# A two-stage graph network on one core: layer 0 taken over its edge blocks as a pipeline, its loads two blocks early, its stores on GpSimd's queue, the first norm ahead of the branch

## The chip, the cores and the metric

The kernel runs on one core of a Trainium2 chip. A core has a matrix engine (TensorE, PE in the profile), a vector engine (VectorE, DVE), a scalar engine (ScalarE, ACT), a general engine (GpSimd, POOL) and a queue engine (SyncE, SP). They work through their own instruction streams in order and wait for each other by semaphores. SBUF is the on-chip memory with 128 partitions, PSUM holds the results of matmuls, and transfers run on 16 shared DMA engines, issued from SP, ACT or POOL. The metric is the device time of one execution in microseconds (us); lower is better.

## The reference

There are 6250 nodes with 64 features and 206250 directed edges, sorted by target node. First a simple graph layer (layer 0) is applied to the normalised nodes, then three attention layers (the transformer convolution) to the normalised result, each with a residual:

```python
h = jnp.maximum(_layernorm(x, axis=-1), 0.0)
# layer 0: a message per edge from the target's own row, mean by target
x_i = x[dst]
msg = jax.nn.relu(jnp.concatenate([x_i, edge_attr], axis=-1) @ W1 + b1)
summed = jax.ops.segment_sum(msg, dst, num_segments=N)
count = jax.ops.segment_sum(jnp.ones(...), dst, num_segments=N)
aggr = summed / jnp.maximum(count, 1.0)[:, None]
out = jax.nn.relu(aggr + (x @ Wres + bres))
# attention, three times (2, 2 and 1 heads)
q = x @ Wq + bq;  k = x @ Wk + bk;  v = x @ Wv + bv
e = eattr @ We
alpha = jnp.sum(q[dst] * (k[src] + e), axis=-1) / jnp.sqrt(C)
m = jax.ops.segment_max(alpha, dst, num_segments=n)
a = jnp.exp(alpha - m[dst])
a = a / (jax.ops.segment_sum(a, dst, num_segments=n)[dst] + 1e-16)
out = jax.ops.segment_sum(a * (v[src] + e), dst, num_segments=n) + x @ Ws + bs
```

Between the attention layers stands a PReLU. All data is float32.

## The kernel before

The edges are padded to 206848 and cut into 101 windows (`NW`) of 2048 edges (`WE`), each of 4 chunks of 512 edges. As edges are sorted by target, the targets of a window lie within 128 consecutive nodes, those of a chunk within 32. `gnn_kernel` checks this on the chip (L94 to L126: `cur` and `prev` hold the target of each edge and of the edge before it, one window per partition, so 101 partitions), writes two tables (`lrow`, an edge's node within its chunk, and `starts`, where a new node begins) to DRAM, and branches: `windows` when the edges fit, which is what runs here, `general` otherwise.

`windows` first makes constants: index rows, `dl` (target within the chunk), block-diagonal weights `w0blk` and `wblk`, the tables of padding rows. Then the norm of x and its projection run over all 49 node blocks of 128 (L311 to L349); the results go to DRAM as `qt[0]` (the projected row, split into three bf16 parts) and `st[0]` (residual and x).

The loop of layer 0 (L357 to L426) goes over the 101 windows. In each: `ea`, the edge features for four windows, is loaded every fourth window (L361); the copy `ead` rearranges the attention's edge features from DRAM to DRAM (L365); `lb` brings `lrow` on 96 partitions (L369), `load_q` the rows of the window's chunks from `qt[0]` (L296), `rx` residual and x (L372). A one-hot matrix `ohT` is made of `lb` (L374) and stored as `ohd` for the attention layers (L375). For two halves of the window, PE forms the messages in `pm` (edge part L380, node part L383), ACT takes the Relu (L387), and PE sums them by node in `acc` with the one-hot `oh` (L389, L400). `nodes` orders the sums by node (L302 to L308), the last node of a window is carried to the next by a matmul with `last` (L393). Then come mean, residual and second norm on DVE and ACT (L405 to L424), and `project` (L275 to L289) makes k, v, q and the skip row and stores them on SP as `kvt`, `qt` and `st`, next to x1 as `x1t` (L411). After the loop `masks` (L235 to L256) makes scans from `starts`.

`attention` runs three times over the 404 chunks. Its `fetch` (L442) collects k and v of 128 source nodes per instruction, four per chunk, by an indirect DMA from POOL, four chunks ahead; `scores`, `rows`, `chain`, `columns` and `sums` do the softmax and the sums, and `project` makes the next layer's rows.

The order of instructions on each engine is set by a scheduler from the order in the source and the readiness of the tiles; pools rotate their buffers (`bufs`), and a load waits until the last reader of its buffer is done. DMAs from SP and ACT take eight semaphores in turn, those from POOL eight of their own, and each waits for the one before it on its semaphore.

The `first_node(wi, c)` that gives the address of a window's rows is read into a register of SP. The lines that carry the loop of layer 0:

```python
for wi in range(NW):
    if wi % 4 == 0:
        ...
    lb = gp.tile([3 * CN, WE], BF16, name="lb0")
    nc.sync.dma_start(lb, lrow[None, wi * WE:(wi + 1) * WE].to_broadcast([3 * CN, WE]))
    q = load_q(gp, 0, wi)
    ...
    win = nodes(wp, mp, acc, wi, D + 1)
    ...
    project(wp, mp, hn, 0, wi)
masks()
```

Of the kernel before, what the change touches and what calls it, by code (L numbers as in the profile page):

```python
# [21 lines left out]
F32 = mybir.dt.float32  # L22
# [6 lines left out]
SP = mybir.EngineType.SP  # L29

# [28 lines left out]

G = 4  # L60
# [4 lines left out]
def gnn_kernel(ctx: ExitStack, tc: tile.TileContext, x, src_t, dst_t, dst_row, ea16, ea32, eaT16, eaT32, w, out):  # L65
    nc = tc.nc
    cp = ctx.enter_context(tc.tile_pool(name="const", bufs=1))
    dr = ctx.enter_context(tc.tile_pool(name="dram", bufs=1, space=bass.MemoryType.DRAM))


    ident = cp.tile([P, P], F32, name="ident")
    make_identity(nc, ident)
    w0 = cp.tile([D + 1, 2 * D], F32, name="w0")
    nc.sync.dma_start(w0[:D, :D], w["L0_gnn_W1"][:D, :])
    nc.sync.dma_start(w0[D:D + 1, :D], w["L0_gnn_b1"][None, :])
    nc.sync.dma_start(w0[:D, D:], w["L0_gnn_Wres"])
    nc.sync.dma_start(w0[D:D + 1, D:], w["L0_gnn_bres"][None, :])
    wl = []
    for l in range(LAYERS):
        t = cp.tile([D + 1, 4 * D], F32, name=f"wl{l}")  # L80
        for i, s in enumerate("qkvs"):
            nc.sync.dma_start(t[:D, i * D:(i + 1) * D], w[f"L1_gnn_W{s}{l}"])
            nc.sync.dma_start(t[D:D + 1, i * D:(i + 1) * D], w[f"L1_gnn_b{s}{l}"][None, :])
        wl.append(t)
    slope = cp.tile([P, 1], F32, name="slope")
    nc.sync.dma_start(slope, w["L1_gnn_prelu_a"][None, :].to_broadcast([P, 1]))


    lrow = dr.tile([EP], BF16, name="lrow")
    starts = dr.tile([EP], BF16, name="starts")  # L90
    base_i = cp.tile([1, NW, WC], I32, name="base_i")
    base = cp.tile([P, NW, WC], F32, name="base")
    with tc.tile_pool(name="chk", bufs=1) as p, tc.tile_pool(name="chkp", bufs=1, space=PSUM) as pp:
        cur = p.tile([NW, WE], I32, name="cur")  # L94
        nc.sync.dma_start(cur, dst_row[1:].rearrange("(w e) -> w e", e=WE))
        prev = p.tile([NW, WE], I32, name="prev")
        nc.scalar.dma_start(prev, dst_row[:EP].rearrange("(w e) -> w e", e=WE))
        after = p.tile([NW, 1], I32, name="after")
        nc.sync.dma_start(after[:NW - 1, :], dst_row[1:].rearrange("(w e) -> w e", e=WE)[1:, 0:1])
        nc.sync.dma_start(after[NW - 1:, :], dst_row[EP:][:, None])  # L100
        ends = p.tile([NW, WC + 1], F32, name="ends")
        nc.vector.tensor_copy(ends[:, :WC], cur.rearrange("w (c e) -> w c e", e=CH)[:, :, 0])
        nc.vector.tensor_copy(ends[:, WC:], after)
        nc.vector.memset(ends[0:1, 0:1], 0.0)
        bad = p.tile([NW, WC + 2], F32, name="bad")
# [20 lines left out]
        nbad_i = cp.tile([1, 1], I32, name="nbad_i")  # L126
# [5 lines left out]
        nc.sync.dma_start(lrow.rearrange("(w e) -> w e", e=WE), lb)  # L132
# [3 lines left out]
        nc.scalar.dma_start(starts.rearrange("(w e) -> w e", e=WE), sb)  # L136

    with tc.If(nc.values_load(nbad_i[0:1, 0:1], min_val=0, max_val=2 * EP) == 0) as fits:
        windows(tc, x, src_t, dst_t, eaT16, eaT32, w, out, ident, w0, wl, slope, lrow, starts, base_i, base)
# [3 lines left out]

@with_exitstack
def windows(ctx: ExitStack, tc, x, src_t, dst_t, eaT16, eaT32, w, out, ident, w0, wl, slope, lrow, starts, base_i,
            base):
# [6 lines left out]
    qt = [dr.tile([NR, 3, D], BF16, name=f"qt{l}") for l in range(LAYERS + 1)]  # L153
    st = [dr.tile([NR, 2 * D if l == 0 else D], F32, name=f"st{l}") for l in range(LAYERS + 1)]
    kvt = [None] + [dr.tile([NR, 2 * D], F32, name=f"kvt{l}") for l in range(1, LAYERS + 1)]
    x1t = dr.tile([NR, D], F32, name="x1t")
    fin = dr.tile([NR, D], F32, name="fin")
    ohd = dr.tile([NW, 3 * CN, WE], BF16, name="ohd")
    ead = dr.tile([NW, P, WC, P], F32, name="ead")
# [28 lines left out]
    none = cp.tile([P, 2 * D], F32, name="none")  # L188
    nc.gpsimd.memset(none, 0.0)
    for l in range(1, LAYERS + 1):  # L190
        nc.scalar.dma_start(kvt[l][N:NP, :], none[:NP - N, :])
        nc.scalar.dma_start(kvt[l][NP:, :], none)

    w0blk = cp.tile([P, 8 * D], F32, name="w0blk")
    nc.gpsimd.memset(w0blk, 0.0)
    for j in range(8):
        nc.scalar.dma_start(w0blk[j * 16:(j + 1) * 16, j * D:(j + 1) * D], w["L0_gnn_W1"][D:, :])
    wblk = []
    for l in range(LAYERS):
        t = cp.tile([P, 4 * D], F32, name=f"wblk{l}")  # L200
        nc.gpsimd.memset(t, 0.0)
        for j in range(4):
            nc.scalar.dma_start(t[j * 32:(j + 1) * 32, j * D:(j + 1) * D], w[f"L1_gnn_We{l}"])
        wblk.append(t)
    srci = cp.tile([P, T], I32, name="srci")
    nc.sync.dma_start(srci, src_t)
# [12 lines left out]
    with tc.tile_pool(name="dsti", bufs=1) as p:  # L219
        dsti = p.tile([P, NW, WT], I32, name="dsti")  # L220
        nc.sync.dma_start(dsti, dst_t.rearrange("p (w t) -> p w t", t=WT))
# [11 lines left out]
    whole = cp.tile([P, NS], F32, name="whole")  # L233

    def masks():  # L235
        nc.vector.memset(keep, -BIG)
        full = GROUPS.count(ST // WT)
        for h in range(2):
            nc.sync.dma_start(keep[h * ST:(h + 1) * ST, :full, :P],
                              starts[:full * ST * P].rearrange("(s r e) -> r s e", r=ST, e=P))  # L240
            for s in range(full, NS):
                n = GROUPS[s] * WT
                nc.sync.dma_start(keep[h * ST:h * ST + n, s, :P],
                                  starts[GW[s] * WE:GW[s] * WE + n * P].rearrange("(r e) -> r e", e=P))
        nc.vector.tensor_copy(new, keep[:, :, 0])
        nc.vector.memset(keep[:, :, 0:1], -BIG)
        zero = cp.tile([P, P], BF16, name="zero")
# [3 lines left out]
        for s in range(NS):  # L251
            nc.vector.tensor_tensor_scan(head[:, s, 1:], zero[:, 1:], keep[:, s, 1:P], 0.0, op0=OP.add, op1=OP.min)
        for s in range(NS):
            nc.vector.tensor_tensor_scan(tail[:, s, P - 2::-1], zero[:, 1:], keep[:, s, P - 1:0:-1], 0.0,
                                         op0=OP.add, op1=OP.min)
        nc.vector.tensor_copy(whole, head[:, :, P - 1])  # L256

    def first_node(wi, c=0):
        return nc.values_load(base_i[0:1, wi, c:c + 1], engines=(SP,), min_val=0, max_val=NP,
                              skip_runtime_bounds_check_because="a node")  # L260

    def parts(wp, q, dest):

        k = len(q.shape) - 1
        at = lambda i: dest[(slice(None),) * k + (i,)]
        nc.scalar.copy(at(0), q)
        r = wp.tile(list(q.shape), F32, name="r_part")
        nc.vector.tensor_sub(r, q, at(0))
        nc.scalar.copy(at(1), r)
        nc.vector.tensor_sub(at(2), r, at(1))  # L270

    def project(wp, mp, h, l, wi):
# [7 lines left out]
        kv = wp.tile([P, 2 * D], F32, name="kv_n")  # L280
        nc.scalar.copy(kv, po[:, D:3 * D])
        q = wp.tile([P, 3, D], BF16, name="q_n")
        parts(wp, po[:, :D], q)
        skip = wp.tile([P, D], F32, name="skip_n")
        nc.scalar.copy(skip, po[:, 3 * D:])
        at = first_node(wi)
        nc.sync.dma_start(kvt[l + 1][bass.ds(at, P), :], kv)
# [24 lines left out]
    with tc.tile_pool(name="n0", bufs=1) as pool, tc.tile_pool(name="n0w", bufs=2) as wp, \  # L312
# [22 lines left out]
        for b0 in range(0, NB, 4):  # L335
            nb = min(4, NB - b0)
            pt = psum.tile([D, 4 * P], F32, name="pr_t")
            for b in range(nb):
                nc.tensor.transpose(pt[:, b * P:(b + 1) * P], hn[:, b0 + b, :], ident)
# [864 lines left out]
```

## Time and profile before

| | |
|---|---|
| median of 3 runs | 9451.41 us (9446.79 to 9455.32) |
| the profiled execution | 7907.74 us |
| its span, first to last instruction | 7906.0 us |
| mean granted clock of TensorE | 0.555 |
| instructions | 99343 |
| PE busy | 4509.4 us |
| DVE busy | 3418.8 us |
| ACT busy | 995.2 us |
| POOL busy | 4717.1 us |

The profile is one execution; the runs are others, and their median lies 1543.67 us above it. Times within the program are those of the profiled execution. A row of a group gives line, engine, operation, output and inputs, the number of instructions, their busy time and the mean of one in ns, then the idle time of the engine just before them and what ended it. In the chain of waits, each step is the work, or the wait, that the end of the program hangs on.

### The profile page before, as it was taken

The page shows a single profiled execution, that of the slowest core. Times are in us where ns is not written, and L with a number is a line of the kernel's source. Part 1 is how long each engine was busy: PE and PEld are TensorE (multiplying, and loading weights), DVE is VectorE, ACT ScalarE, POOL GpSimd, SP SyncE. Part 2 cuts the span into 40 slices and gives each one's busy share as a digit, 9 for nine tenths or more (in the row PEclk, how much of TensorE's full clock was granted, in tenths as well). Part 3 has the DMA queues.
Part 4 walks back from the last instruction along what each step waited for, and adds up shares of the span by engine and source line. Part 5 has one row for each costly group of instructions (what it writes and reads, how often), then busy time and mean ns, then how long its engine had stood idle before and what let it go on. Part 6 is the DMA issues. An engine that isn't in the chain of part 4 may idle for free.

```text
span 7906.0 us, 99343 instructions
## 1 busy us (share of the span) xinstructions
PE 4509.4 (57%) x26120; PEld 3054.7 (39%) x26120; DVE 3418.8 (43%) x11804; ACT 995.2 (13%) x4565; POOL 4717.1 (60%) x5248
## 2 busy tenths in 40 slices
PE   1555555546666666665566666666645555555555
PEld 1333333324444444443344444444433333333333
DVE  2322332344444444444444444445444444444444
ACT  0222222201111111111011111111110000000001
POOL 0000000067777777775777777777757777777775
PEclk9866676755555555555555555555555555555555
DMA  1544333333333333332333333333323333333333
GB/s 47 165 134 114 87 92 88 88 93 98 94 97 97 96 95 97 97 97 74 94 94 96 97 94 97 97 97 94 97 71 93 93 92 90 93 93 93 90 93 77
DMA packets 778275, 748.00 MB, mean 95 GB/s; under 512 B 474481, under 2 KB 612179, under 8 KB 777469
## 3 DMA queue, kind: packets, MB, share of 16 engines
q1 hardware_dynamic: 545096, 352.43, 16.3%
q0 software_dynamic: 155136, 318.03, 16.1%
q10 hardware_dynamic: 77471, 71.10, 3.2%
q8 instruction: 214, 3.51, 0.2%
q14 instruction: 358, 2.93, 0.1%
HBM read 643.14 MB, written 125.88 MB: 97 GB/s over the span
## 4 chain that ended last, share of the span: by engine, by line
DMA 26%; POOL 26%; issue 21%; PE 12%; DVE 11%; ACT 2%; SPq 2%; ACTq 0%; DVEq 0%; POOLq 0%
POOL kv L442 26%; DMA kv<-kvt,srci 21%; PE pm L380 3%; DVE kv L475 3%; PE acc L400 2%; PE po L279 2%; DVE prod L477 1%; DMA ead<-in_eaT_dram 1%; DMA q<-qt 1%; PE acc L592 1%; ACT msg L387 1%; PE pe L469 1%; PE pt L275 1%; PE pm L383 1%; DVE hn L616 1%
## 5 line engine op out<-in xcount | busy, mean ns | idle before, releaser
L442 POOL DMA_INDIRECT kv<-kvt,srci x4848 | 4648.1, 959 | 1514.4 <-issue 1239.2
L469 PE MATMUL pe<-wblk,ea 128*128 128x256 f32 x2424 | 1436.7, 696 | 2213.3 <-DVE kv L475 1833.6
L475 DVE TENSOR_TENSOR kv<-kv,pe 128x512 f32<-128x512 f32 x1212 | 832.8, 687 | 3080.2 <-DMA kv<-kvt,srci 2971.3
L469 PEld LDWEIGHTS pe<-wblk,ea 128*128 128x128 f32 x2424 | 626.9, 312 | 2466.9 <-DVE kv L475 2055.3
L592 PE MATMUL acc<-u,oh 128*32 128x66 f32 (+1 forms) x9090 | 1257.0, 315 | 208.6 <-DVE oh L582 198.1
L592 PEld LDWEIGHTS acc<-u,oh 128*32 128x32 f32 x9090 | 932.1, 165 | 390.4 <-DVE oh L582 281.7
L386 POOL MEMSET msg<- 128x8 f32 x202 | 23.8, 119 | 1357.0 <-PE acc L394 969.6
L472 PEld LDWEIGHTS <-ohT 96*128 96x128 bf16 x4848 | 480.4, 138 | 454.9 <-issue 344.4
L472 PE MATMUL pq<-q,ohT 96*128 96x64 bf16 x4848 | 528.7, 245 | 14.3 <-DMA q<-qt 10.3
L578 DVE TENSOR_TENSOR u<-kv,ex 128x256 f32<-128x256 f32 x1212 | 506.1, 418 | 15.4 <-ACT ex L554 9.6
L477 DVE TENSOR_TENSOR prod<-kv,pq 128x256 f32<-128x256 f32 x1212 | 495.4, 409 | 4.1
L479 DVE TENSOR_REDUCE al<-prod 128x8 f32<-128x256 f32 (+1 forms) x1212 | 495.7, 410 | 1.1
L577 ACT COPY u<-ex 128x8 f32<-128x8 f32 (+1 forms) x1212 | 225.9, 199 | 1788.2 <-PE acc L592 997.4
L380 PE MATMUL pm<-w0blk,ea 128*128 128x512 f32 x404 | 305.8, 863 | 172.0 <-DMA ea<-in_eaT_dram 118.9
L279 PE MATMUL po<-wl,ht 65*128 65x256 f32 x606 | 355.5, 688 | 36.4 <-ACT ht L277 35.6
L582 DVE TENSOR_TENSOR oh<-row,dl 128x128 f32<-128x128 f32 x1212 | 340.3, 281 | 6.0 <-PE acc L592 3.4
L306 PE MATMUL pn<-sums,of 128*128 128x65 f32 (+1 forms) x808 | 251.0, 410 | 72.4 <-ACT sums L302 72.1
L400 PE MATMUL acc<-msg,oh 128*32 128x65 f32 x3030 | 225.7, 265 | 104.9 <-ACT msg L387 81.7
L306 PEld LDWEIGHTS pn<-sums,of 128*128 128x128 f32 x808 | 197.8, 292 | 172.4 <-ACT sums L302 142.4
L400 PEld LDWEIGHTS acc<-msg,oh 128*32 128x32 f32 x3030 | 185.7, 136 | 170.1 <-issue 136.6
L389 DVE TENSOR_TENSOR oh<-row,dl 128x256 f32<-128x256 f32 x202 | 85.6, 424 | 364.0 <-PE acc L400 186.5
L302 ACT COPY sums<-acc 128x65 f32<-128x65 f32 (+1 forms) x404 | 86.9, 215 | 1219.1 <-PE acc L592 1081.6
(172 smaller groups left out, 3800.5 us busy)
## 6 DMA issues: line engine op xcount, KB each, us to landing
ohT<-ohd SPq DMA_DIRECT2D x303, 384.0 KB
kv<-kvt,srci POOLq DMA_INDIRECT x4848
ea<-ead SPq DMA_DIRECT2D x303, 256.0 KB
lb<-lrow SPq DMA_DIRECT2D x101, 384.0 KB
ohd<-ohT ACTq DMA_DIRECT2D x101, 384.0 KB
ead<-in_eaT_dram ACTq DMA_DIRECT2D x404, 64.0 KB
q<-qt SPq DMA_DIRECT2D x1616, 12.0 KB
kvt<-kv_n SPq DMA_DIRECT2D x303, 64.0 KB
```

Of the source, the lines that this page charges most:

```text
L279: nc.tensor.matmul(po, ht, wl[l], start=True, stop=True)
L306: nc.tensor.matmul(pn, of, s, start=True, stop=True)
L380: nc.tensor.matmul(pm, ea[:, wi % 4, u, :], w0blk, start=True, stop=False)
L400: nc.tensor.matmul(acc[c * CN:(c + 1) * CN, :], oh[:, j, :], msg[:, j, :], start=(j % 4 == 0), stop=(j % 4 == 3))
L442: nc.gpsimd.indirect_dma_start(out=t[:, j, :], out_offset=None, in_=kvt[l + 1][:, :], in_offset=bass.IndirectOffsetOnAxis(ap=srci[:, 4 * c ...
L469: nc.tensor.matmul(pe.rearrange("p j f -> p (j f)"), ea[:, k, :], wblk[l], start=True, stop=True)
L472: nc.tensor.matmul(pq[:, j, :], ohT[:, (4 * k + j) * P:(4 * k + j + 1) * P], q[:, k, :], start=True, stop=True)
L475: nc.vector.tensor_add(both, both, pe[:, :, None, :].to_broadcast([P, 4, 2, D]))
L477: nc.vector.tensor_mul(prod, kv[:, :, :D], pq)
L479: nc.vector.tensor_reduce(als[s][:, :, t0:t0 + 4].rearrange("p h j -> p j h"), prod.rearrange("p j (h c) -> p j h c", h=H), axis=AX.X, op= ...
L578: nc.vector.tensor_mul(u[:, :, :D].rearrange("p j (h c) -> p j h c", h=H), kv[:, :, D:].rearrange("p j (h c) -> p j h c", h=H), e[:, :, :, ...
L592: nc.tensor.matmul(acc[k * CN:(k + 1) * CN, :], oh[:, j, :], u[:, j, :], start=(j == 0), stop=(j == 3))
```

## The change

What it does:

- The norm of x and its projection move into `gnn_kernel`, ahead of the branch, in groups of 12 or 13 node blocks; x is laid out with 49 consecutive nodes per partition; the Relu is taken by ACT on the transposed block, and each group is stored on its own as `q0` and `rx0`.
- `cur`, `prev`, `lrow` and `starts` are moved as 96 and 5 partitions instead of 101; the column `after` comes from a matmul with a shifted identity instead of two loads. The small weights are loaded on GpSimd's and ACT's queues instead of SP's.
- Layer 0 becomes a loop of stages: `load0` two windows ahead, `spread`, `collect` one behind, `join` and `finish` two behind, `put` three behind. `pm` is a single tile of two PSUM banks, with the edge part as four matmuls of 64 rows; three fixed `msgs` replace the memset per half window. Pools have three buffers, `rx` five.
- k, v, skip and x1 of a node are one row of a table `tab` (256 floats); layer 0 stores it and `q` from GpSimd, later layers from SP. `fetch` reads the first half of a row, by doubled indices.
- The copy `ead` is gone; the attention layers load `ea` from `eaT32` for four windows at once.
- The scans of `masks` stand within the loop of layer 0, one group at a time.

The diff, cut:

```diff
+        most = slice(0, NW // 16 * 16)
+        rest = slice(NW // 16 * 16, NW)
+        for r in (most, rest):
+            nc.sync.dma_start(cur[r], by_window(dst_row[1:])[r])
+            nc.scalar.dma_start(prev[r], by_window(dst_row[:EP])[r])
+        xs = pool.tile([P, NB, D], F32, name="xs")
+        nc.sync.dma_start(xs, x.rearrange("(p b) f -> p b f", b=NB))
...
+                nc.gpsimd.dma_start(wl[l][:D, i * D:(i + 1) * D], w[f"L1_gnn_W{s}{l}"])
...
+        nc.tensor.matmul(pa, ident[:NW, 1:NW + 1], first, start=True, stop=True)
...
+        for g0 in range(0, NB, 12):
...
+                nc.scalar.activation(hT[:D, :nb * P], pt[:, :nb * P], AF.Relu)
...
+                parts(nc, wp, po[:, :nb, :D], q[:, b1])
+                nc.scalar.copy(rx[:, b1, :D], po[:, :nb, D:])
+            nc.gpsimd.tensor_copy(rx[:, g0:g1, D:], xg)
+            nc.sync.dma_start(to_q[:, g0:g1], q[:, g0:g1])
+            nc.sync.dma_start(to_rx[:, g0:g1], rx[:, g0:g1])
...
-    srci = cp.tile([P, T], I32, name="srci")
-    nc.sync.dma_start(srci, src_t)
...
     def project(wp, mp, h, l, wi):
...
-        kv = wp.tile([P, 2 * D], F32, name="kv_n")
-        nc.scalar.copy(kv, po[:, D:3 * D])
+        rows = rows_n[wi % 3]
+        nc.scalar.copy(rows[:, :SKIP + D], po[:, D:])
...
-        nc.sync.dma_start(kvt[l + 1][bass.ds(at, P), :], kv)
-        nc.sync.dma_start(qt[l + 1][bass.ds(at, P)], q)
-        nc.sync.dma_start(st[l + 1][bass.ds(at, P), :], skip)
+        e, engine = (nc.gpsimd, POOL) if l == 0 else (nc.sync, SP)
+        at = first_node(wi, engine=engine)
+        e.dma_start(tab[l + 1][bass.ds(at, P), :], rows)
+        e.dma_start(qt[l + 1][bass.ds(at, P)], q)
...
-            for j in range(4):
-                nc.scalar.dma_start(
-                    ead[wi, j * 32:(j + 1) * 32],
-                    eaT32[:, wi * WE:(wi + 1) * WE].rearrange("k (c j e) -> k c j e", j=4, e=P)[:, :, j])
...
+        def spread(wi):
...
+            pm = pp.tile([P, 2, 2, 4, D], F32, name="pm")
+            for u in range(2):
+                for r in range(2):
+                    h = slice(r * D, (r + 1) * D)
+                    nc.tensor.matmul(pm[:, r, u].rearrange("p j f -> p (j f)"), ea[h, wi % 4, u, :], w0blk[h, :],
+                                     start=(u == 0), stop=False)
...
+            msg = msgs[wi % 3]
+            for r in range(2):
+                nc.scalar.activation(msg.rearrange("p (u r j) f -> p r u j f", u=2, r=2)[:, r, :, :, :D], pm[:, r],
+                                     AF.Relu)
...
+        for wi in range(2):
+            load0(wi)
+        nc.sync.dma_start(srci, src_t)
+        nc.vector.tensor_single_scalar(srci, srci, 1, op=OP.logical_shift_left)
+        load_masks()
+        for wi in range(NW + 4):
+            if wi + 2 < NW:
+                load0(wi + 2)
+            if wi < NW:
+                spread(wi)
+            if 0 <= wi - 2 < NW:
+                join(wi - 2)
+            if 0 <= wi - 1 < NW:
+                collect(wi - 1)
+            if 0 <= wi - 2 < NW:
+                finish(wi - 2)
+            if 0 <= wi - 3 < NW:
+                put(wi - 3)
+            if wi % 2 == 1 and wi // 2 - 2 in range(NS):
+                masks(wi // 2 - 2)
...
-                    out=t[:, j, :], out_offset=None, in_=kvt[l + 1][:, :],
+                    out=t[:, j, :], out_offset=None, in_=tab[l + 1].rearrange("n (i f) -> (n i) f", i=2),
...
-            ea = gp.tile([P, WC, P], F32, name="ea")
-            nc.sync.dma_start(ea, ead[wi])
+            if wi % 4 == 0:
+                n = min(4, NW - wi)
+                ea = gp.tile([P, 4, WC, P], F32, name="ea")
+                for j in range(4):
+                    nc.sync.dma_start(
+                        ea[j * 32:(j + 1) * 32, :n],
+                        eaT32[:, wi * WE:(wi + n) * WE].rearrange("k (w c j e) -> k w c j e", c=WC, j=4, e=P)[:, :, :, j])
```

## The prediction

> **What bounds the kernel now.** I read the busy table first, then the time by stage, the chain of waits in order of time, the waits of the layer-0 loop, and last the timeline of one block there. From the page, the span, the granted clock, the chain by line and the fetch row:
>
> ```profile
> span 7906.0 us, 99343 instructions
> PEclk9866676755555555555555555555555555555555
> DMA 26%; POOL 26%; issue 21%; PE 12%; DVE 11%; ACT 2%; SPq 2%; ACTq 0%; DVEq 0%; POOLq 0%
> ...
> L442 POOL DMA_INDIRECT kv<-kvt,srci x4848 | 4648.1, 959 | 1514.4 <-issue 1239.2
> ```
>
> The fetch row runs in the three attention layers alone. 4648.1 us busy and 1239.2 us of gaps that wait for nothing make 1.21 us for each of 4848 fetches. Busy time by stage (start-up, layer-0 loop, attention 1 to 3; columns: length, busy of PE, PE load, DVE, ACT, POOL, clock, DMA share, GB/s):
>
> ```profile
> 0.00:240.00 240.00, 36.08 (x157) 31.48 (x157) 54.35 (x105) 22.05 (x43) 13.41 (x37) 1.00 0.26 72
> 240.00:1616.00 1376.00, 797.58 (x5957) 478.64 (x5957) 421.34 (x1614) 303.16 (x1111) 23.60 (x199) 0.69 0.38 106
> 1616.00:3700.00 2084.00, 1271.58 (x6757) 871.73 (x6757) 1015.34 (x3523) 255.32 (x1287) 1558.55 (x1668) 0.51 0.37 95
> ```
>
> Attention is bound by POOL: 1558.6 of 2084 us busy, PE and DVE well below. An attention layer makes 1616 fetches in about 2097 us (6290/3), 1.30 us each. Layer 0 has no such bound: of 1376 us PE is busy 58%, DVE 31%, ACT 22%, DMA 38%. The chain of waits in order of time shows the start-up as five single transfers:
>
> ```profile
> 0.83 33.50 DMA prev<-in_dst_row_dram
> 44.87 34.62 DMA cur<-in_dst_row_dram
> 90.93 30.60 DMA starts<-sb
> 133.53 10.24 DMA xs<-in_x_dram
> 205.97 22.41 DMA qt<-q
> ```
>
> They are 131.4 us of the 240. In the loop, the waits between 700 and 1500 us (57.5 blocks; total, times, longest):
>
> ```profile
> ACT msg L387 <- PE pm L383: 218.7, 58, 9.9
> ...
> DVE ohT L374 <- DMA lb<-lrow: 104.5, 15, 7.4
> ...
> PE pm L380 <- DMA ea<-in_eaT_dram: 99.0, 15, 7.0
> ```
>
> Every fourth block waits about 7 us for its loads, and every block waits for its own chain. The timeline gives the same matmul at two rates:
>
> ```profile
> 799.73 1.12 PE L380 MATMUL pm<-w0blk,ea 128*128 128x512 f32 x2
> ...
> 824.32 3.75 PE L380 MATMUL pm<-w0blk,ea 128*128 128x512 f32 x4 [6.59 <-DMA ea<-in_eaT_dram]
> ```
>
> 0.56 us without a stall, 0.94 after one: the stall costs its own length and then a slow clock.
>
> **What the Trainium skill says.** "TensorE: Matmul & The Clock Gate", Part 1: the matmul clock is either half or full, decided by how busy the array was in windows of about 3.4 us. The trace agrees: 0.69 in layer 0 as a mixture, 0.51 in attention. "DMA: Bandwidth & Descriptors", section "Why a DMA increments its semaphore by 16 and not by 1": a transfer from SP or ACT is spread over the largest number of DMA engines, at most 16, that divides its outermost size; 101 rows leave one. The trace agrees: cur, 808 KB on 101 partitions, took 34.62 us (24 GB/s), xs, 1.6 MB on 128 partitions, 10.24 us. "TensorEngine Tiling (Array Packing)", Performance Considerations: a contraction of at most 64 rows leaves room for two matmuls side by side. No row of before shows it.
>
> **The change part by part, against the profiled execution.**
>
> *Start-up, 240 us to about 105.* cur and prev become 96 rows on 16 engines and 5 rows on five, issued at once with xs. 3.2 MB at the 213 GB/s that the stretch 200 to 225 us reached are 15 us; cur and prev first, so the checks begin near 10 us instead of 79.5. They last 11.4 us of DVE (79.5 to 90.9). The norm then costs DVE 4 x 3.42 us, and the parts of 13 groups 2 x 0.42 us each, 11 us; PE needs 5.4 us for 8 node blocks (175.9 to 181.3), 33 us, the longest of the three; with 12 us before its first transpose it ends near 70. POOL now issues 25 weight loads ahead of the memsets of hT: at 1.3 us (the fetch pace) 33 us, inside that. Stores go out by quarters; the last 1.5 MB at 213 GB/s take 7 us and a landing. From the branch to the first layer-0 matmul: constants 12 us (121.7 to 133.5) with srci (808 KB), dsti and the first loads beside and after them, some 12 more. Sum 105; bounds 90 and 135. Saved: 135.
>
> *The layer-0 loop, 13.6 us a block to about 7.5.* PE: 797.6/101 = 7.9 us a block at clock 0.69, so 5.45 at full clock and 10.9 at half. The four pm matmuls cover the same columns as before (2 x 512 = 4 x 256 on half the rows); side by side they would save half of 2.95 us at 0.69 (171.3/58), 1 us at full clock. I take nothing and keep 1 for the range. The order of the changed program on PE decides what remains exposed: after the 16 ohT matmuls of a block come the acc matmuls of that same block, so PE still waits for two Relu of 0.60 us, about 1.3 us with the hand-over; the pn, pt and po of earlier blocks now stand between ohT matmuls, where they wait little, 0.3 us for ht. So 5.45 + 1.6 = 7.05 us at full clock, 12.5 at half. With short gaps alone I expect full clock nine tenths of the time: 7.05 x 0.9 + 12.5 x 0.1 = 7.6; 7.5 taken.
> The other engines in a block: DVE 421.3/101 = 4.2 us plus the mask scans, 56 x 0.33 us (11 in 3.62), 0.2 a block, though they stand bunched in its first blocks; ACT 3.0; SP issues lb, four q with a register load each (2.8 us per four), rx and two ea, about 4.5, and no longer waits behind stores (x1t and kvt held SP 174.1 and 68.2 us of 800). The stores, one row of 1 KB per node and q, go to POOL, idle there (23.6 of 1376 us): two issues at 1.3 us. Queued behind a waiting POOL store is only the next block's. DMA: 384 KB each for lb and ohd, 128 for ea, 176 for stores, 112 for q and rx, 1.18 MB a block; at 90 GB/s and a share of 0.32 the engines could move 281 GB/s, 4.2 us. The ead copy (256 KB in and out per block) is gone. None reaches 7.5. SP and ACT issue transfers in turn on eight counters, so one waits for the eighth before it; at nine transfers a block, landing in 2 to 4 us (lb 3.5, q 2 to 3.2), the counters allow a block per 3 us, but the first load behind eight ea waits for the ohd before, which eats part of the two-block lead every fourth block. That is why I don't go below 7.
> 101 x 7.5 = 758, and 12 us for the last block to leave the pipeline: 770 against 1376. Saved: 606. Bounds for a block: 6.0 (pm side by side, always full clock) and 10.5 (clock mostly half).
>
> *Attention: nothing.* ea comes straight from eaT32 in 512-byte runs, 1 MB every fourth block instead of 256 KB each block; the same bytes, at 281 GB/s 3.7 us of engine time in a lead of one block (20.8 us). The row fetch has the same count and size (512 bytes), every second 512 bytes of a table of 1 KB rows. Fetches are issued four chunks ahead (some 20 us), and POOL waits for its transfers 78.3 us in all, so a slower landing has room. Bounds -40 and +60 us. The masks no longer stand behind the loop; they were hidden under the first fetches.
>
> Sum: 135 + 606 = 741, so 7908 - 741 = 7167 us for the profiled execution.
>
> **From this execution to the median.** The profiled execution took 7907.74 us, the median of the runs is 9451.41, 1543.7 more, and no view says where. If that lies outside layer 0 (in the POOL fetches it would be 0.32 us each), the gain stays 741: 8710. If it is spread over everything, factor 1.195, the gain is 886: 8565. I take 8650.
>
> **Rivals.**
> *Loop stays at 10.5 us a block* (counters and the remaining chain leave PE at half clock; for it: the clock is 0.51 at 61% busy in attention; against it: the chain per block on PE gets shorter by all but the Relu). Loop 1072, saved 439 in all: 9012, or 8926 with the factor; about 8970.
> *Loop falls to 6.0 us* (pm side by side and full clock). Loop 618, saved 893: 8558, or 8384; about 8470.
> *The interleaved table slows the fetch.* This ends on the other side. Place: 4848 fetches on POOL, the bound of 80% of the span. It decides from 741/4848 = 0.153 us a fetch; at 0.25 us it costs 1212 us: 9451 + 1212 - 741 = 9922. For it: nothing else in the change can cost this much. Against it: equal size, equal count, equal lookahead.
> *No net change*: the attention waits for layer 0's stores on POOL and the loop's lead is lost in full; around 9450.
>
> **How the numbers follow.** Forecast 0.55, 10.5 us loop 0.20, 6.0 us loop 0.20, slow fetch 0.04, no change 0.01. The forecast alone spans 8490 to 8790 (block 6.8 to 8.2, and both readings of the gap). Up to 8900 it takes in most of the slow loop, down to 8430 most of the fast one. Within 0.2% is about what this measurement can't tell from no change; faster 0.95, same 0.01, slower 0.04.
>
> **What would show it.** First layer-0 matmul near 105 us; first fetch near 875; clock in the loop above 0.85 and blocks 7 to 8 us apart; cur landing within 10 us; the fetch row still x4848 at 959 ns. I am wrong if the fetch row's mean or its gaps grow, if the loop's clock stays near 0.7, or if PE waits for lb or ea at every fourth block as long as before.

## The result, and the profile after

| | before | after |
|---|---|---|
| median of 4 runs | 9451.99 us (9446.79 to 9455.32) | 9748.01 us (9743.68 to 9757.75) |
| profiled execution | 7907.74 us | 9757.75 us |

The ratio is 1.0315, 95% interval [1.0297, 1.0333]: slower, where 8650 us and a gain were foretold. One thing has to be said before any of these numbers can be read: the kernel before takes 9450 to 9590 us on some chips ("at 9450" below) and 7900 to 7920 us on others ("at 7908"), and the profile from which the prediction was worked out came from an execution of the second kind, the medians from the first. Every experiment is set against the kernel before on its own chip. The experiments met each of their six chips once; whether it is the chip or the time of the run that decides, and what makes the difference, no run shows.

First the page of the changed kernel at 9450 (span, clock in 40 slices, the chain by engine, the row fetch):

```profile
span 9755.6 us, 95919 instructions
PEclk6666555555555555555555555555555555555555
another core or an unknown queue 34%; PE 19%; DVE 13%; issue 12%; POOL 5%; ACT 2%; DMA 2%; ACTq 0%; SPq 0%; DVEq 0%; POOLq 0%
L507 POOL DMA_INDIRECT kv<-tab,srci x4848 | 4703.0, 970 | 3333.5 <-issue 1289.1
```

The fetches cost what they cost before (970 ns against 959), and as much "issue" between them. What has grown is the rest of POOL's idle time before them, 2044 us of 3333.5 against 275 of 1514.4: POOL stands and waits for buffers that the other engines free. A third of the chain can't be traced to a releaser; why is said below, where the engines stand still. The busy time by stage (start-up, layer-0 loop, attention 1 and 2; length, busy PE, PE load, DVE, ACT, POOL, clock, DMA share, GB/s) says where:

```profile
0.00:110.00 110.00, 41.45 (x232) 34.33 (x233) 55.92 (x143) 27.89 (x72) 42.77 (x87) 0.75 0.51 142
110.00:1005.00 895.00, 700.06 (x6299) 508.04 (x6296) 401.96 (x1550) 284.48 (x1007) 109.29 (x205) 0.61 0.46 137
1005.00:3800.00 2795.00, 1038.69 (x6335) 705.63 (x6334) 962.15 (x3208) 220.45 (x1091) 1568.67 (x1643) 0.55 0.28 69
3800.00:6700.00 2900.00, 1134.74 (x6807) 769.66 (x6807) 1028.55 (x3488) 243.95 (x1204) 1592.57 (x1675) 0.55 0.27 69
```

The first fetch stands at 1009 us instead of 1616: start-up and layer 0 did give 607 us. But an attention layer now takes 2894 to 2940 us (from first fetch to first fetch, the last one to the end), 8747 us for the three. PE has less to do in it than in the 2084 us of the layer shown of before (1039 and 1135 us against 1272), the other engines about as much.

### The profile page after: what moved, and what is told of

Same layout as the page of the kernel before. It is cut to its first block, busy times and chain, and to the rows that moved or that the text cites. A ratio compares the mean times of both kernels' runs of the same rounds, so it can differ in the third digit from the quotient of the medians.

```text
span 9755.6 us, 95919 instructions
## 1 busy us (share of the span) xinstructions
PE 3926.3 (40%) x26529; PEld 2737.0 (28%) x26529; DVE 3476.1 (36%) x11720; ACT 952.9 (10%) x4287; POOL 4891.4 (50%) x5305
## 4 chain that ended last, share of the span: by engine, by line
another core or an unknown queue 34%; PE 19%; DVE 13%; issue 12%; POOL 5%; ACT 2%; DMA 2%; ACTq 0%; SPq 0%; DVEq 0%; POOLq 0%
PE pe L541 6%; PE acc L664 5%; POOL kv L507 5%; DVE prod L549 2%; DVE kv L547 2%; DVE al L551 2%; PE pq L544 2%; PE po L342 2%; PE pn L367 1%; DVE u L650 1%; DMA kv<-tab,srci 1%; DVE oh L654 1%; PE pr L571 1%; PE acc L658 1%
## 5 line engine op out<-in xcount | busy, mean ns | idle before, releaser
L507 POOL DMA_INDIRECT kv<-tab,srci x4848 | 4703.0, 970 | 3333.5 <-issue 1289.1
L541 PE MATMUL pe<-wblk,ea 128*128 128x256 f32 x2424 | 1237.6, 626 | 1349.6 <-DVE kv L547 1057.0
L664 PE MATMUL acc<-u,oh 128*32 128x66 f32 (+1 forms) x9090 | 1048.9, 303 | 1370.8 <-DVE oh L654 579.3
L664 PEld LDWEIGHTS acc<-u,oh 128*32 128x32 f32 x9090 | 826.0, 159 | 1506.5 <-issue 1060.3
L541 PEld LDWEIGHTS pe<-wblk,ea 128*128 128x128 f32 x2424 | 574.5, 286 | 1647.0 <-DVE kv L547 1129.0
L544 PE MATMUL pq<-q,ohT 96*128 96x64 bf16 x4848 | 436.0, 230 | 884.9 <-DVE prod L549 478.4
L544 PEld LDWEIGHTS <-ohT 96*128 96x128 bf16 x4848 | 370.5, 124 | 1169.6 <-issue 1061.3
L349 POOL DMA_DIRECT2D tab<-rows x101 | 54.7, 541 | 756.8 <-ACT q_n L212 711.6
L342 PE MATMUL po<-wl,ht 65*128 65x256 f32 x606 | 322.5, 630 | 239.4 <-ACT ht L340 160.8
L340 ACT COPY ht<-pt 64x128 f32<-64x128 f32 x303 | 78.3, 258 | 1857.0 <-PE pt L338 1382.4
```

The source lines that it names most:

```text
L342: nc.tensor.matmul(po, ht, wl[l], start=True, stop=True)
L507: nc.gpsimd.indirect_dma_start(out=t[:, j, :], out_offset=None, in_=tab[l + 1].rearrange("n (i f) -> (n i) f", i=2), in_offset=bass.Indire ...
L541: nc.tensor.matmul(pe.rearrange("p j f -> p (j f)"), ea[:, wi % 4, k, :], wblk[l], start=True, stop=True)
L544: nc.tensor.matmul(pq[:, j, :], ohT[:, (4 * k + j) * P:(4 * k + j + 1) * P], q[:, k, :], start=True, stop=True)
L664: nc.tensor.matmul(acc[k * CN:(k + 1) * CN, :], oh[:, j, :], u[:, j, :], start=(j == 0), stop=(j == 3))
```

## The experiments

Times of a stage are read from each trace: the first fetch ends layer 0, attention is the rest. Ratios are to before on the same chip; except for the last run, each is one execution.

| run | this | before | ratio | attention |
|---|---|---|---|---|
| e0_before | 9588 | 9579 | 1.001 | 7971 |
| e1_ead | 9004 | 9579 | 0.940 | 7914 |
| e2_tables | 10094 | 9579 | 1.054 | 9081 |
| e3_both | 9012 | 9579 | 0.941 | 7938 |
| e4_short_runs | 8936 | 9459 | 0.945 | 7852 |
| e5_bursts | 8882 | 9459 | 0.939 | 7802 |
| e6_by_window | 9876 | 9459 | 1.044 | 8867 |
| e7_more_packets | 8918 | 9459 | 0.943 | 7833 |
| e8_own_table | 7415 | 7912 | 0.937 | 6363 |
| e9_four_transfers | 7467 | 7912 | 0.944 | 6387 |
| e10_pause | 8387 | 7912 | 1.060 | 7311 |
| e11_gate | 7512 | 7912 | 0.949 | 6424 |
| e12_after | 7377 | 7908 | 0.933 | 6365 |
| e13_own_table | 7416 | 7908 | 0.938 | 6366 |
| e14_gate | 7509 | 7908 | 0.950 | 6419 |
| e15_own_table | 9782 | 9465 | 1.033 | 8726 |
| e16_gate | 8884 | 9465 | 0.939 | 7803 |
| e17_four_transfers | 7471 | 7906 | 0.9445 [0.9429, 0.9461] | 6384 |

### Which part of the change loses the time

The kernel before once more, for a profile that goes with its median; then the change with the copy `ead` put back, with the separate tables put back, and with both.

> The kernel before, unchanged, to have a profile that goes with the median of its runs. All theories: about 9452 us. Theory E (edge features) and theory T (row table): if its start-up and layer 0 take 1616 us as in the profile shown of before, its three attention layers take about 7836 us, 2612 each, 515 us more per layer than in that profile, with PE, DVE and ACT standing idle together in stretches of 5 to 25 us as they do after the change, but in fewer of them. Theory S (spread): the missing 1544 us lie in layer 0 as well, so that layer 0 takes 1616 x 1.195 = 1930 us and an attention layer 2507 us.

The page of this run and two of its stages (layer-0 loop, attention 1):

```profile
span 9585.9 us, 99343 instructions
L442 POOL DMA_INDIRECT kv<-kvt,srci x4848 | 4657.8, 961 | 3120.7 <-issue 1273.1
...
L277 ACT COPY ht<-pt 64x128 f32<-64x128 f32 x303 | 78.5, 259 | 2260.4 <-remote 1905.2
```

```profile
240.00:1616.00 1376.00, 794.71 (x5957) 477.83 (x5957) 421.94 (x1614) 303.28 (x1111) 24.16 (x200) 0.69 0.38 106
1616.00:4300.00 2684.00, 1212.00 (x6810) 827.63 (x6810) 1004.47 (x3543) 245.86 (x1302) 1565.37 (x1671) 0.54 0.27 74
```

Start-up and layer 0 are those of the profile at 7908: the first fetch stands at 1615 us against 1616, the loop has 794.71 us of PE against 797.58 and the clock 0.69 in both. All that is missing lies in attention: 7971 us against 6290. So theory S is out, and the first of the two readings in the prediction was the right one for the gain in layer 0. The edit of e1, in `load0` and in the `load` of attention:

```diff
+            for j in range(4):
+                nc.scalar.dma_start(
+                    ead[wi, j * 32:(j + 1) * 32],
+                    eaT32[:, wi * WE:(wi + 1) * WE].rearrange("k (c j e) -> k c j e", j=4, e=P)[:, :, j])
...
-            if wi % 4 == 0:
...
+            ea = gp.tile([P, WC, P], F32, name="ea")
+            nc.sync.dma_start(ea, ead[wi])
```

> The changed kernel with the copy of the edge features put back: four copies a block from ACT's queue in layer 0, one load a window from it in attention. Theory E (the attention layers lose because ea now comes as 1 MB every fourth window in 512-byte runs): attention falls from 8750 us to about 7836, the whole to about 8850 us (layer 0 some 20 us longer with the copies). Theory T (they lose because k, v, skip and x1 share a table of 1 KB rows): nothing gained, 9750 to 9800 us. Theory N (neither; the attention is slower because of when or where the program runs it): 9700 to 9850 us.

> The changed kernel with the tables of before: kvt, skip rows and x1 apart, four stores a block in layer 0 (on GpSimd's queue) and three in attention (on SP's), indices not doubled. Theory T: attention falls from 8750 us to about 7836, the whole to about 8830 us. Theory E: nothing gained, about 9750 us, layer 0 up to 100 us longer by the two further stores on GpSimd. Theory N: 9700 to 9850 us.

> The changed kernel with both put back, so that the attention layers are those of before and only the start-up and the pipeline of layer 0 are new. Theories E and T: about 8850 us, the better of the two runs with one part put back. Theory N: 9700 to 9850 us, attention still about 2900 us a layer.

The part of e2 and e3 with the tables, cut (stores in `project`, fetch, index):

```diff
-        e.dma_start(tab[l + 1][bass.ds(at, P), :], rows)
+        e.dma_start(kvt[l + 1][bass.ds(at, P), :], kv)
         e.dma_start(qt[l + 1][bass.ds(at, P)], q)
+        e.dma_start(skt[l + 1][bass.ds(at, P), :], skip)
...
+            nc.gpsimd.dma_start(x1t[bass.ds(first_node(wi, engine=POOL), P), :], x1)
...
-        nc.vector.tensor_single_scalar(srci, srci, 1, op=OP.logical_shift_left)
...
-                    out=t[:, j, :], out_offset=None, in_=tab[l + 1].rearrange("n (i f) -> (n i) f", i=2),
+                    out=t[:, j, :], out_offset=None, in_=kvt[l + 1][:, :],
```

e1 takes 9004 us, 0.940 of before: attention falls to 7914. Theory E holds. Layer 0 ends at 1088 us instead of 1009 in the changed kernel: the copies cost 79 us there, not 20. With the tables put back as well (e3) attention is 7938, the same. Only with ea from the input do the separate tables matter, and then the other way round from theory T: e2 takes 1.054 of before where the changed kernel takes 1.0315. That is one execution, and why the further stores weigh only there wasn't tried.

### What about these loads costs

A window's ea comes in 128 runs of 2 KB from the copy, in 512 runs of 512 bytes from the input, there 1 MB at once every fourth window, in four transfers into 32 partitions each, from 32 rows 827 KB apart. Four kernels change one of these each: e4 lays the copy out with the chunk ahead of the partition, e5 loads four windows of the copy at once, e6 is the changed kernel with one window at a time from the input, e7 is e1 with a load that nobody reads. The cuts of e4, e5 and e7 are against e1, that of e6 against the changed kernel.

```diff
-    ead = dr.tile([NW, P, WC, P], F32, name="ead")
+    ead = dr.tile([NW, WC, P, P], F32, name="ead")
...
-            nc.sync.dma_start(ea, ead[wi])
+            nc.sync.dma_start(ea, ead[wi].rearrange("c k e -> k c e"))
```

```diff
-            nc.sync.dma_start(ea, ead[wi])
+            if wi % 4 == 0:
+                n = min(4, NW - wi)
+                ea = gp.tile([P, 4, WC, P], F32, name="ea")
+                nc.sync.dma_start(ea[:, :n], ead[wi:wi + n].rearrange("w k c e -> k w c e"))
```

```diff
-                        ea[j * 32:(j + 1) * 32, :n],
-                        eaT32[:, wi * WE:(wi + n) * WE].rearrange("k (w c j e) -> k w c j e", c=WC, j=4, e=P)[:, :, :, j])
+                    ea[j * 32:(j + 1) * 32],
+                    eaT32[:, wi * WE:(wi + 1) * WE].rearrange("k (c j e) -> k c j e", c=WC, j=4, e=P)[:, :, j])
```

```diff
+            idle = gp.tile([3 * CN, WC, D], BF16, name="idle")
+            nc.sync.dma_start(idle, qt[l + 1][:P].rearrange("(c n) i f -> (n i) c f", c=WC))
```

> The kernel with the copy put back (9004 us, attention 7914), with the copy laid out so that a window's load is one transfer of 256 KB in 512 runs of 512 bytes instead of 128 runs of 2 KB. Theory P (what costs is the number of short runs, that is of DMA packets, on SP's queue during attention): attention about 8750 us as in the changed kernel, the whole about 9840 us. Theory B (the burst of 1 MB every fourth window): unchanged, about 9000 us. Theory D (the source in DRAM, 32 rows 827 KB apart): unchanged, about 9000 us.

> The kernel with the copy put back, but the attention loads four windows of it at once, 1 MB in runs of 2 KB every fourth window. Theory B: attention about 8750 us, the whole about 9840 us. Theory P: as many runs as with the copy loaded by window, about 9000 us. Theory D: about 9000 us.

> The changed kernel without the copy, but the attention loads the features of one window at a time straight from the input, 512 runs of 512 bytes in four transfers of 64 KB. Theory B: attention back to about 7914 us, the whole about 8920 us. Theories P and D: as the changed kernel, about 9750 us.

> The kernel with the copy put back, and one more transfer a window in the attention layers that nobody reads: 384 runs of 128 bytes, 48 KB. It has as many packets as the changed kernel and 208 KB a window less than another load of features would bring. Theory P: attention about 8750 us, the whole about 9840 us. Theories B and D: 9000 to 9050 us.

Runs as short as the input's (e4: attention 7852), bursts (e5: 7802) and 384 more packets a window (e7: 7833) cost nothing against 7914 of e1 (on a chip slower by 1.3%). One window at a time from the input (e6) is as slow as four: 8867. Packets and bursts are out. So is the number of issues on SP: the changed kernel issues as many loads of ea in attention as e1 does (312 against 303) and loses, and e6 issues four times as many and is 1.4% slower in attention than the changed kernel. Nor are the packets themselves slow where time is lost: those of 512 bytes lasted 28 ns on average in e6 as in e4, and in the changed kernel 45 ns at 9450 as at 7908.

e8 copies the input in layer 0 to a table `eac` of the same layout and loads from that; e9 is e1 with the window's load cut in four (its edit is against e1, that of e8 against the changed kernel).

```diff
+    eac = dr.tile([32, EP], F32, name="eac")
...
+            nc.scalar.dma_start(eac[:, wi * WE:(wi + 1) * WE], eaT32[:, wi * WE:(wi + 1) * WE])
...
-                        eaT32[:, wi * WE:(wi + n) * WE].rearrange("k (w c j e) -> k w c j e", c=WC, j=4, e=P)[:, :, :, j])
+                        eac[:, wi * WE:(wi + n) * WE].rearrange("k (w c j e) -> k w c j e", c=WC, j=4, e=P)[:, :, :, j])
```

```diff
-            nc.sync.dma_start(ea, ead[wi])
+            for j in range(4):
+                nc.sync.dma_start(ea[j * 32:(j + 1) * 32], ead[wi, j * 32:(j + 1) * 32])
```

> The changed kernel with its four transfers of 1 MB per four windows, but from a table of the kernel's own that has the layout of the input (32 rows 827 KB apart) and is copied from it in layer 0, one copy of 256 KB a block. Theory D (the rows far apart): attention stays near 8750 us, the whole near 9800 us. Theory I (it is the input's own place in DRAM): attention about 7900 us, the whole about 8950 us. Theory F (four transfers into 32 partitions each): as theory D.

> The kernel with the rearranged copy put back, runs of 2 KB, but a window's 256 KB are loaded in four transfers into 32 partitions each, as the loads from the input are. Theory F: attention about 8800 us, the whole about 9850 us. Theories D and I: attention about 7900 us, the whole about 8950 us, at most 60 us a layer more for three further issues a window on SP.

Both met a chip at 7908, where the two forms take almost the same (6363 and 6387 us). The first was run twice more, the second once:

> The kernel with the features in a table of its own in the layout of the input. On a chip where before takes about 9450 us: theories D (rows far apart) and F (four transfers into 32 partitions each) 9800 us, attention about 8750; theory I (the input's own place) about 8950 us, attention about 7900. Where before takes about 7910 us: 7415 us as before, and no theory is told apart.

> The kernel with the features in a table of its own in the layout of the input. On a chip where before takes about 9450 us: theories D (rows far apart) and F (four transfers into 32 partitions each) 9800 us, attention about 8750; theory I (the input's own place) about 8950 us, attention about 7900. Where before takes about 7910 us: 7415 us.

> The rearranged copy, runs of 2 KB, a window's 256 KB loaded in four transfers into 32 partitions each. On a chip where before takes about 9450 us: theory F (the form of the transfers) about 9850 us, attention about 8750; theory D (rows far apart) about 8950 us, attention about 7900, at most 60 us a layer more for three further issues a window on SP. Where before takes about 7910 us: 7467 us, and the two stay open.

e13 met 7908 again (7416). e15 met a chip at 9450: attention 8726, as slow as from the input. So it isn't the input's own place in DRAM (theory I is out). e17 met 7908 once more and says nothing on the point. Whether it is the rows far apart (D) or the four transfers into 32 partitions (F) is left open.

### Does the changed kernel lose where before takes 7908 us

> The changed kernel, unchanged. On a chip where before takes about 9450 us: 9750 us, attention about 8750 us (all theories). On one where it takes about 7910 us: if the loss from the loads of ea needs the standstill of the other engines, as I now hold, attention stays at 6300 to 6450 us and the whole is 7300 to 7450 us, near the 7167 that was foretold for the profiled execution; if the loads cost by themselves, attention is about 7100 us and the whole about 8100 us.

It takes 7377 us, 0.933 of before. Its page and its stages, on the same borders as above as far as the first fetch:

```profile
span 7374.9 us, 95919 instructions
...
POOL 24%; DMA 21%; PE 18%; issue 17%; DVE 16%; ACT 3%; SPq 1%; DVEq 0%; POOLq 0%; another core or an unknown queue 0%; ACTq 0%
...
L507 POOL DMA_INDIRECT kv<-tab,srci x4848 | 4706.3, 971 | 1483.4 <-issue 1187.2
```

```profile
0.00:110.00 110.00, 42.12 (x244) 34.48 (x245) 57.05 (x146) 28.15 (x72) 43.44 (x87) 0.79 0.50 144
110.00:1005.00 895.00, 701.43 (x6281) 509.07 (x6281) 400.73 (x1546) 284.36 (x1006) 109.31 (x205) 0.61 0.46 137
1005.00:3100.00 2095.00, 1115.27 (x6638) 751.56 (x6639) 1005.39 (x3395) 232.17 (x1157) 1580.99 (x1669) 0.56 0.38 95
```

The same instructions, and the same start-up and loop to 2 us. In attention the fetches stand with little gap but "issue", POOL is again the head of the chain, and everything is traced. So the loss needs both: 9450, and the loads of ea in the form that they have from the input.

### How the engines stand still, and a theory on it whose forecast failed

A stretch of e0 (timeline; start, length, engine):

```profile
3040.23 6.14 SPq L296 DMA_DIRECT2D q<-qt  x4
...
3044.44 0.42 PE L275 MATMUL pt<-ident,hn 128*64 128x128 f32 x1
...
3045.33 0.41 DVE L479 TENSOR_REDUCE al<-prod 128x8 f32<-128x256 f32 x1
3046.34 0.95 POOL L442 DMA_INDIRECT kv<-kvt,srci  x1 [0.30 <-issue]
3047.59 0.94 POOL L442 DMA_INDIRECT kv<-kvt,srci  x1 [0.30 <-issue]
...
3055.09 0.95 POOL L442 DMA_INDIRECT kv<-kvt,srci  x1 [0.30 <-issue]
3057.75 0.26 ACT L277 COPY ht<-pt 64x128 f32<-64x128 f32 x1 [15.92 <-remote]
3058.06 1.22 PE L279 MATMUL po<-wl,ht 65*128 65x256 f32 x2 [12.40 <-ACT ht L277]
```

PE transposes h into `pt` at 3044.4. ACT, which has nothing else to do, copies it 13 us later, and PE and DVE wait for that. POOL meanwhile fetches at its pace of 1.25 us. SP needs 6.14 us for four loads of q; in the profile at 7908 the same four took 2.79:

```profile
3008.94 2.79 SPq L296 DMA_DIRECT2D q<-qt  x4
```

The trace shows why: in between, many of SP's register instructions, mostly 0.03 to 0.05 us long and 0.27 for a load, last about 0.70 us (1082 of 6429 lasted 0.65 or more in the attention of e0, none of 6434 in the profile at 7908). How much the others get done while POOL fetches without a pause can be counted: from 5 us after the start of such a stretch, DVE starts 1.6 instructions per us at 7908; at 9450 it is 0.78 in e0, 0.74 in e1 and 0.41 in the changed kernel.

The traces say one step more about what is waited for. They hold the time at which each semaphore went up, a record that no view lists. In layer 0, PE's semaphore goes up 0.014 us (median) after the end of the matmul that raises it, at 7908 and at 9450. In attention at 7908, no such record stands over 1 us behind PE's last signalling matmul before the program's closing steps. In e0, 1753 of 5323 stand more than 2 us behind, up to 23 us. For DVE there are 6 such records, for ACT none. The copy at 3057.75 started 0.06 us after one of them, and of 643 waits of ACT and DVE on PE's semaphore of over 5 us, 437 ended within 0.15 us of one. So the others stood waiting for signals of PE that came late. Whether the matmul or its signal was late can't be said, as the ends of matmuls are modelled. The changed kernel has the same at 9450 (1379 of 5987, up to 40 us).

The traces at 9450 also lack records: in attention 5513 of DVE's 9956 semaphore records are there in e0, 9872 in the profile at 7908; in layer 0 both have all 1717. Untraced waits ("remote", "another core or an unknown queue") are therefore in part missing records. That points to a rival that no run separates: the recording itself may hold the engines up. Every time on record comes with a span and a clock, so none is known to be free of it.

The counts of DVE suggested a theory, S in the expectations that follow (another than the spread above): the unbroken sequence of fetches holds the others up. Both start from e5: e10 puts a memset after every fourth fetch, e11 lets each chunk's fetches wait for a product of DVE.

```diff
+        pause = gp.tile([P, 1024], F32, name="pause", bufs=1)
...
+            nc.gpsimd.memset(pause, 0.0)
             kvs[c] = t
```

```diff
             if c + AHEAD < NCH:
+                if c > 0:
+                    nc.gpsimd.tensor_copy(gate, state["prod"][0:1, 0, 0:1])
                 fetch(c + AHEAD)
```

> The kernel with the rearranged copy, loaded for four windows at once (8882 us), with a memset of 128x1024 on GpSimd after every fourth fetch, by estimate 1 us each from 0.88 us for the copy of 128x832 there: 1212 us more for GpSimd. Theory S (while GpSimd issues fetch after fetch, the other engines get on at a third of their rate, and a pause lets them go on): the memsets replace waits, attention falls from 7802 to 7300-7600 us, the whole to about 8400-8700 us. Theory C (the stalls have to do with the amount of fetches only, not with their sequence): up to 600 us more, about 9000 to 9500 us.

> The same kernel with no memset, but a copy of one element on GpSimd ahead of each chunk's four fetches that waits for DVE's product of an earlier chunk, so that GpSimd is at most five chunks (20 fetches, 25 us) ahead of DVE. Theory S: long runs of fetches past DVE stop, attention 7200 to 7600 us, the whole 8300 to 8700 us. Theory C: a further wait on the engine that bounds, 8900 to 9200 us.

> The rearranged copy, loaded for four windows at once, with the wait for DVE's product ahead of each chunk's fetches. On a chip where before takes about 9450 us: theory S (standstill while GpSimd issues fetch after fetch) 8300 to 8700 us, attention 7200 to 7600; theory C (the sequence doesn't matter) 8850 to 9150 us, attention 7800 to 8000. Where before takes about 7910 us: 7512 us as before, and nothing is told apart.

> The rearranged copy, loaded for four windows at once, with the wait for DVE's product ahead of each chunk's fetches. On a chip where before takes about 9450 us: theory S (standstill while GpSimd issues fetch after fetch) 8300 to 8700 us, attention 7200 to 7600; theory C (the sequence doesn't matter) 8850 to 9150 us, attention 7800 to 8000. Where before takes about 7910 us: 7510 us.

e10, e11 and e14 met 7908. There the pause costs most of its price: 1212 memsets of 969 ns are 1174 us, on the engine that bounds, and attention is 7311 us, 946 more than the 6365 of the changed kernel. With the gate attention is 6424 and 6419 us, where the copy with four loads a window has 6387 and 6384. e16 met a chip at 9450 and took 8884 us, attention 7803, against 8882 and 7802 of the same kernel without the gate (e5, on a chip at 9459). Its rows on POOL:

```profile
L513 POOL DMA_INDIRECT kv<-tab,srci x4848 | 4702.8, 970 | 1820.1 <-issue 1197.2 <-DVE z L690 317.6 <-DVE oh L660 159.3
L540 POOL COPY gate<-prod 1x1 f32<-1x1 f32 x1197 | 234.8, 196 | 808.2 <-DVE prod L554 759.3 <-DVE z L690 17.2 <-issue 5.9
```

The gate did hold POOL back (808.2 us before it, and the longest stretch of fetches fell from 121 to 61 us). The wait moved from the buffers to the gate, and the time stayed. So the forecast that went with the theory failed, and a gate that lets POOL run 20 fetches ahead is no remedy. The theory itself isn't refuted: of the 1059 signals of PE that came over 5 us late in e0, 74% came while POOL was between two fetches more than 0.5 us apart, which it is for 24% of the time. That fits a standstill that lasts as long as POOL fetches, but POOL's stops can also be its consequence. The pause was never tried at 9450. What makes PE's signals late stays open, and so does why the loads of ea in the input's form make the time longer still.

## Why the prediction was wrong, step by step

**Start-up, 240 to 105: right, a little better.** The first layer-0 matmul stands at 89 us, 1 us under the lower bound; saved 152. cur had landed by 13.6 us, not within 10, against 79.5 before. That agrees with the Trainium skill, "DMA: Bandwidth & Descriptors", section "Why a DMA increments its semaphore by 16 and not by 1": 96 rows go over 16 engines where 101 went over one.

**The layer-0 loop, 7.5 us a block: right in three blocks of four.** 75 blocks are 7.5 us apart on average, every fourth 12.9 (between the Relu of one block and the next; 12.7 to 13.0 apart from the first and last). That is 25 x 5.4 = 135 us of the 151 by which the loop's gain, 455 us, missed 606. Two blocks of e12 in the timeline:

```profile
503.77 1.57 PE L407 MATMUL pm<-w0blk,ea 64*128 64x256 f32 x8
...
508.59 1.23 PE L436 MATMUL acc<-msg,oh 128*32 128x65 f32 x11 [1.32 <-ACT msg L417]
...
515.80 0.96 PE L436 MATMUL acc<-msg,oh 128*32 128x65 f32 x11 [1.32 <-ACT msg L417]
```

```profile
516.97 6.73 SPq L386 DMA_DIRECT2D ea<-in_eaT_dram  x8
...
523.04 1.23 PE L436 MATMUL acc<-msg,oh 128*32 128x65 f32 x11 [1.94 <-ACT msg L417]
...
528.25 2.93 PE L407 MATMUL pm<-w0blk,ea 64*128 64x256 f32 x10
...
531.79 1.22 PE L407 MATMUL pm<-w0blk,ea 64*128 64x256 f32 x2
...
533.27 1.22 PE L407 MATMUL pm<-w0blk,ea 64*128 64x256 f32 x4
...
535.72 1.23 PE L436 MATMUL acc<-msg,oh 128*32 128x65 f32 x11 [0.69 <-ACT msg L417]
```

The sums of a block begin 7.2 us apart. While the eight transfers of ea for the next four windows are issued (6.73 us on SP), PE has no edge matmuls; in the block after that it does those of two blocks, sixteen instead of eight, and 12.7 us pass. The prediction named the eight ea transfers as a reason not to go below 7 and gave them no term of their own. That it was PE's fixed order and not the landing that put them together is my reading of the trace; no kernel tried it.

**The clock: wrong.** Full clock was expected nine tenths of the time; it was 0.61 in the loop, lower than the 0.69 of before, though PE was busy for 78% of it (700 of 895 us) against 58%; why, no run shows. What made up for it is the term that I had taken at nothing: eight edge matmuls on 64 rows took 1.57 us above, and 1.13 at best in the loop, where before four on 128 rows took 2 x 1.12. That agrees with the Trainium skill, "TensorEngine Tiling (Array Packing)", Performance Considerations.

**Attention, "nothing" with bounds of -40 and +60 us: this is the step that failed.** At 7908 it nearly holds, 15 us past its bound: 6365 us against 6290, of which the fetch row explains 58 (970.8 instead of 958.8 ns, 4848 times). At 9450 the sentence that failed is "the same bytes, at 281 GB/s 3.7 us of engine time in a lead of one block": it priced the loads of ea by their bytes and their own lateness. Their packets aren't slow there and nothing was shown to wait for them in particular; with them, the work beside them gets slower. The cost, from before at 9450 (9452 - 1616 - 2 for what lies around the span = 7834 us) to 8747, is 913 us. 913 - 607 = 306 us of loss, and 296 were measured. With any rearranged copy the attention of the changed kernel is 7802 to 7914 us.

**From this execution to the median: the question was put and then passed over.** I asked where the 1544 us lay and carried on with the gain alone. The right reading (outside layer 0) was among the two, but both took for granted that what lay there would not answer to the change. For the profiled execution itself, 7167 us was foretold and 7377 measured: the direction holds, the size is 531 of 741.

**The rivals.** The one that ended on the other side had the right place, attention, and the wrong mechanism: the fetch's mean hardly grew (970 ns against 959). The signs of being wrong did come: the idle time before the fetches grew, and the clock of the loop stayed low. "Equal size, equal count, equal lookahead" was right and no protection. "Nothing else in the change can cost this much" was the wrong sentence.

**A version that beats both at 9450.** In one execution each, the changed kernel with the copy put back: 0.940 of before (e1), 0.939 with four windows of the copy loaded at once (e5). At 7908 the copy with four loads a window keeps 0.9445 [0.9429, 0.9461]; there the changed kernel is a little better (0.933, one execution): without the copies its layer 0 ends at 1010 us instead of 1085.

## What to carry to other kernels

When one profile and the median of the runs differ by a sixth, take a profile that goes with the median before pricing anything: the stage that holds the difference is the one in which a change can do what the profile doesn't show. A load that is "the same bytes, only laid out otherwise" is worth a run with the old layout kept; here, at 9450, it took back the whole gain of a pipeline that did what it was meant to. And a load issued for several blocks at once needs a term of its own in the sum, for the block in which it falls.

## What the runs showed of the hardware that was not expected

- The same program takes 7908 us on one chip and 9450 to 9590 on another, all of it in the stages with back-to-back fetches (attention 6290 against 7971 us), while layer 0 agrees to 2 us.
- There, PE, DVE and ACT stood still together for 5 to 20 us while POOL issued fetches undisturbed, and one in six of SP's register instructions took about 0.70 us instead of 0.03 to 0.27. A third of PE's recorded semaphore updates came over 2 us late (1753 of 5323), almost none of DVE's and ACT's.
- Loads of ea from 32 rows 827 KB apart, in four transfers into 32 partitions each, cost some 900 us more there in 303 windows than a compact copy (913 against before; 8867 against 7852 us of attention in e6 and e4, whose packets both took 28 ns).
